# Four cross-attention and mixture-of-experts layers: layer 0's attention in a written TensorE order, and layer 1's setup and row gathers moved

## The chip, the cores and the metric

The kernel runs on one core of one Trainium2 chip. The metric is device time in microseconds of one execution; five runs of the kernel before gave 1270.8 to 1281.63 us with a median of 1277.07 us.

## The reference, cut to what matters

The input x is 4 batches of 512 tokens by 128 features, the context is 4 batches of 154 rows by 128, all float32. Four layers follow each other:

```python
for layer in range(4):
    x = x + attention[layer](layernorm(x), context)
    x = x + experts[layer](layernorm(x))
```

Layer 0's attention compares each token with the context rows, and projects four features:

```python
Sim  = (h @ w1)[:, :, None] + (c @ w2)[:, None, :] + einsum('bid,bjd->bij', h * w3, c) + b_sim
hq   = softmax(Sim, 2) @ c                       # per token
hc   = softmax(max(Sim, 2), 1) @ h               # one row per batch
out  = concat([h, hq, h * hq, h * hc]) @ W_qv + b_qv
```

Layer 1 is masked attention with 16 heads of 8 features; layers 2 and 3 have 16 heads of 64. Each expert layer has 8 experts with 512 or 256 hidden features. Layers 0, 2 and 3 send each token to the two experts with the highest gate logits and add the two results with softmax weights; layer 1 sends it to one, with a capacity of 321 tokens an expert.

## The kernel before, in words

x stays in SBUF, four tiles (one a batch) of 128 partitions by 4 groups of 128 tokens. Tokens are routed in two halves, batches 0 and 1 and batches 2 and 3.

**Layer 0's attention** (`attend_first`). `prepare(b)` normalises a batch, transposes it, multiplies it with the context (L1006) and makes the softmax's exponents on ScalarE (L1021). `tile_of` then transposes the probabilities (L1033, L1038; evacuated as `pm` and `pt`), multiplies them with the context (`hq`, L1041 and L1042), takes the maximum of the batch through a transpose and a matmul by ones (L1048, L1051, `m0`, `mall`), makes `md` (L1054), an exponent `ebt` (L1057) and the batch's row `hc` (L1060, L1061, `hd`, `hr`, `hc`, `wc` L1070), and projects the features in 12 matmuls (L1078, `res` L1081, added to x in L1083). The order of all this, on every engine, is found by a scheduler that lists instructions by its own estimate of times.

**The route of a half** (`route`, a generator that is advanced in steps): statistics and normalisation (L227 to L243; `rstd` L236 runs on GpSimd), transposes (L251), gating logits `lg` (L666, L672), the two best experts (`top`, `sel` L687), each token's rank within its expert by nine matmuls (L693, L695) and their copy `rk` (L697), and from it the row of a buffer in DRAM at which the token belongs, `su` (L717). The half's experts fill up to 23 blocks of 128 such rows (15 in layer 1), and `eb` (L745) is each block's expert. The tokens go there by indirect DMAs on GpSimd (L722), 16 in each half of a layer with two choices, 128 rows each. `row_transfers(n, behind)` (L641) issues the next n of these and makes them wait for one instruction, so that they spread over other work; in layer 0 it is called behind `pm`, `pt`, the copy `ft` of `hq`, and `res`, with n = 2.

**Experts** (`experts`). For each block the expert's weights are loaded by SP (L869, three buffers), and for each four blocks the tokens (L840), which wait until all scatters of their half have landed. Tokens are transposed (L850), multiplied with the first weights (L877), activated, multiplied with the second (L916) and stored (L928). A second half's route is advanced between the first half's blocks.

**Gather and combine.** When a half's blocks are stored, 16 indirect DMAs on GpSimd (L953) fetch each token's result rows; `combine` (L971) adds them to x with their weights. Layer 0's second half is gathered and combined beside layer 1's attention (`attend_all`): there the order of TensorE and ScalarE is written out by hand in periods, one for each of 16 tiles of 128 tokens (`narrow_period`; `nm` L294 is the maximum of six heads' scores, `probs` L308 their exponents, `short` L319 the last ScalarE step of a period, `pT` L264 an evacuation of transposed exponents). VectorE's order is the scheduler's. The combining of batches 2 and 3 is spread over the periods from the third tile on, two groups of 128 tokens in each.

**Layer 1's setup** (`layer1_setup`, L1088 on) makes block-diagonal weights through three 8-row transposes (L1099) and the transposed output projection (L1108). It is called right after layer 0's attention, so the scheduler may place it there. Its `prepare(0)`, which loads the mask `mi` and turns it to `madd` (L1122), is called after the first half's experts and gathers.

Of the kernel before, what the change touches and what calls it, by code (L numbers as in the profile page):

```python
# [29 lines left out]
NH = NT // 2  # L30
EPS = 1e-5
NEG = -1e20
BLK = (2 * NH + E - 1, NH + E - 1)
UPS = (2, 1, 1, 1)
NF = (4, 4, 2, 4)
PER = (1, 2, 2, 2)


# [9 lines left out]
def tile_xattn_moe_stack(ctx: ExitStack, tc: tile.TileContext, a: dict, out: bass.AP):  # L48
# [101 lines left out]
    for base, sign in ((0, 1), (D // H - 1, -1)):  # L150
# [17 lines left out]
    fill = const.tile([P, E, NH], F32, name="fill")  # L168
    nc.gpsimd.iota(
        fill, pattern=[[0, E], [P, NH]], base=0, channel_multiplier=0, allow_small_or_imprecise_dtypes=True  # L170
# [6 lines left out]
    nth = const.tile([1, BLK[0], E], F32, name="nth")  # L177
    nc.gpsimd.iota(
        nth, pattern=[[1, BLK[0]], [0, E]], base=0, channel_multiplier=0, allow_small_or_imprecise_dtypes=True
# [59 lines left out]
    def norm(src, found, pool=None):  # L239
        mv, rstd = found  # L240
        xn = (pool or xnp).tile([P, NI, D], F32, tag="xn", name="xn", bufs=3 if pool else 2)
        for i in range(NI):
            nc.vector.tensor_scalar(  # L243
                xn[:, i, :], src[:, i, :], mv[:, i, 0:1], rstd[:, i : i + 1], ALU.subtract, ALU.mult
            )
        return xn
# [23 lines left out]
    class Tile:  # L270
# [31 lines left out]
        def exp(self, g):  # L302
            if g == 0:
                self.pr = p2.tile([P, H, S2], F32, tag="probs", name="probs")
            for s in range(min(3, 8 - 3 * g)):
                for j in range(2):
                    h = self.at.heads(None, 3 * g + s, j)
                    nc.scalar.activation(  # L308
# [5 lines left out]
                    )  # L314

# [44 lines left out]
        def take_ends(self, engine):  # L360
            self.tails = p2.tile([self.rows, 4, P], F32, tag="tails", name="tails")
            copy(engine, self.tails.rearrange("p g q -> p (g q)"), self.q["ends"][0 : self.rows, :])
# [173 lines left out]
    def attention64(b, gather_x, wq, wk, wv, wo, add):  # L536
# [36 lines left out]
        def values_ends():  # L573
# [3 lines left out]
            for r in range(2):  # L577
                rows = slice(64 * r, 64 * r + 64)
                nc.tensor.matmul(q[rows, :], ct2[:, b], wv[:, r * 512 : (r + 1) * 512], start=True, stop=True)
# [6 lines left out]
            at.vt = at.vt.rearrange("p c s d -> p (c s d)")  # L586

# [35 lines left out]
    def rsm(name, *shape, dt=F32):  # L623
        return rt.tile([P, *shape], dt, tag=name, name=name)

    def top(lg):

        m = rt.tile([P, NH], F32, tag="m", name="m", bufs=4)
        nc.vector.tensor_reduce(m, lg, AX.X, ALU.max)
        eq = rt.tile([P, NH, E], F32, tag="eq", name="eq", bufs=4)  # L630
        nc.vector.tensor_tensor(eq, lg, bc(m, 2, E), ALU.is_equal)
        nc.vector.tensor_tensor(eq, eq, bc(rev_e, 1, NH), ALU.mult)
        r = rt.tile([P, NH], F32, tag="r", name="r", bufs=4)
        nc.vector.tensor_reduce(r, eq, AX.X, ALU.max)
        oh = rt.tile([P, NH, E], F32, tag="oh", name="oh", bufs=4)
# [5 lines left out]
    def row_transfers(n=2 * NH, behind=None):  # L641
# [9 lines left out]
    def route(layer, half, wg, bg, b2):  # L651

        lg = rsm("lg", NH, E)
        found = [stats(x[2 * half + k]) for k in range(B // 2)]
        yield
        xns = [norm(x[2 * half + k], found[k], rt) for k in range(B // 2)]
        yield  # L660
        xnTs = [transposed(xn) for xn in xns]
        yield
        for k, xnT in enumerate(xnTs):
            q = ps_tr()
            for i in range(NI):
                nc.tensor.matmul(q[:, i * E : (i + 1) * E], xnT[:, i * P : (i + 1) * P], wg, start=True, stop=True)  # L666
            o = lg[:, k * NI : (k + 1) * NI, :]
            qv = q[:, 0 : NI * E].rearrange("p (i e) -> p i e", i=NI)
            if bg is None:
                nc.vector.tensor_copy(o, qv)  # L670
            else:
                nc.vector.tensor_tensor(o, qv, bc(bg, 1, NI), ALU.add)  # L672
        yield
# [3 lines left out]
        sel = rsm("sel", NH + 1, E, dt=BF16)  # L677
        nc.vector.memset(sel[:, NH, :], 0.0)
        if layer == 1:
            nc.vector.tensor_copy(sel[:, 0:NH, :], oh1)  # L680
        else:
            yield
            lg2 = rsm("lg2", NH, E)
# [3 lines left out]
            nc.vector.tensor_tensor(sel[:, 0:NH, :], oh1, oh2, ALU.add)  # L687
# [3 lines left out]
        n = (NH + 1) * E  # L691
        q = ps_tr()
        nc.tensor.matmul(q[:, 0:n], before, sf, start=True, stop=False)  # L693
        for s in range(1, NH + 1):
            nc.tensor.matmul(q[:, s * E : n], ones_b, sf[:, 0 : n - s * E], start=False, stop=(s == NH))  # L695
        rk = rsm("rk", NH + 1, E)
        nc.vector.tensor_copy(rk, q[:, 0:n].rearrange("p (t e) -> p t e", t=NH + 1))  # L697
        tot = rk[:, NH, :]
        t3 = rsm("t3", E, NH)
        nc.vector.tensor_tensor(t3, bc(tot, 2, NH), fill, ALU.is_gt)  # L700
        nb = rsm("nb", E)
        nc.vector.tensor_reduce(nb, t3, AX.X, ALU.add)
        t4 = rsm("t4", E, E)
# [4 lines left out]
        base = rsm("base", NH, E)  # L708
        nc.vector.scalar_tensor_tensor(base, bc(first, 1, NH), float(P), rk[:, 0:NH, :], ALU.mult, ALU.add)
        slots = []  # L710
        for k, oh in enumerate(ohs):
            t5 = rsm("t5", NH, E)
            nc.vector.tensor_tensor(t5, base, oh, ALU.mult)
            sl = rsm(f"sl{k}", NH)
            nc.vector.tensor_reduce(sl, t5, AX.X, ALU.add)
            su = rsm(f"su{k}", NH, dt=U32)
# [17 lines left out]
        rows_due.extend(partial(scatter, t, su) for t in range(NH) for su in slots)  # L734
        yield

        nj = BLK[layer == 1]
        end = rt.tile([1, E], F32, tag="end", name="end")
        nc.vector.tensor_tensor(end, first[0:1], nb[0:1], ALU.add)
        t6 = rt.tile([1, BLK[0], E], F32, tag="t6", name="t6", bufs=1)  # L740
        nc.vector.tensor_tensor(t6[:, 0:nj, :], bc(end, 1, nj), nth[:, 0:nj, :], ALU.is_le)
        ef = rt.tile([1, BLK[0]], F32, tag="ef", name="ef")
        nc.vector.tensor_reduce(ef[:, 0:nj], t6[:, 0:nj, :], AX.X, ALU.add)
        eb = rt.tile([1, BLK[0]], I32, tag="eb", name="eb")
        nc.vector.tensor_scalar(eb[:, 0:nj], ef[:, 0:nj], float(E - 1), None, ALU.min)  # L745

        if layer == 1:

            le = rsm("le", NH, E)
            nc.vector.tensor_tensor(le, lg, bc(m1, 2, E), ALU.subtract)  # L750
            nc.scalar.activation(le, le, AF.Exp)
            ls = rsm("ls", NH)
            nc.vector.tensor_reduce(ls, le, AX.X, ALU.add)
            cw = rsm("cw", NH)
            nc.vector.reciprocal(cw, ls)
            rg = rsm("rg", NH, E)
            if half:
                nc.vector.tensor_tensor(rg, rk[:, 0:NH, :], bc(seen[0], 1, NH), ALU.add)
                nc.vector.tensor_tensor(rg, rg, oh1, ALU.mult)
            else:  # L760
                seen.append(tot)
                nc.vector.tensor_tensor(rg, rk[:, 0:NH, :], oh1, ALU.mult)
# [670 lines left out]
```

## Time and profile before

| | us |
|---|---|
| median of 5 runs (lowest, highest) | 1277.07 (1270.8, 1281.63) |
| the profiled execution's own time | 1273.25 |
| its span, first to last instruction | 1271.6 |
| TensorE busy | 1079.5 (85%) |
| VectorE busy | 731.1 (57%) |
| ScalarE busy | 565.5 (44%) |
| GpSimd busy | 253.0 (20%) |
| mean granted TensorE clock | 0.923 |

The profile is of one execution. Its time is 1.65 us longer than its span, and 3.82 us below the median of the five runs. A row of the trace gives the start and the duration of an instruction in us, engine (PE is TensorE, DVE is VectorE, ACT is ScalarE, POOL is GpSimd, SPq and POOLq their sequencers), line, operation, output and inputs, how many rows were taken together, and in brackets how long the engine was idle before it and which instruction's end ended that. The granted clock is the share of full speed that the throttle lets TensorE run at.

The stages as the trace has them: layer 0's attention and the first half's route until the first expert matmul at 104.06 us; layer 0's 46 expert blocks until 256 us; layer 1's first tiles, beside which the second half is gathered, until about 330 us; and the rest.

### The profile page before, as it was taken

To read this page: it belongs to the slowest core of one execution; us is meant where nothing else is said; L and a number is where in the kernel's file an instruction comes from. 1 tells how busy PE (TensorE), PEld (TensorE's weight loads), DVE (VectorE), ACT (ScalarE), POOL (GpSimd) and SP (SyncE) were. 2 spreads that over 40 slices of the span, in tenths; PEclk is the share of its full clock that TensorE was granted. 3 is DMA by queue.
4 is the path that set the end of the run, shared out by engine and by line. 5 is a ranking of instruction groups with operands and counts; after the bars stand their busy time and mean duration, and the time that the engine had idled before them with its cause. 6 is when DMAs were issued, how large, how long until landed. Compare 5 with 4: busy or idle time off the path is not lost.

```text
span 1271.6 us, 26318 instructions
## 1 busy us (share of the span) xinstructions
PE 1079.5 (85%) x9351; PEld 887.5 (70%) x9351; DVE 731.1 (57%) x2012; ACT 565.5 (44%) x2264; POOL 253.0 (20%) x281
## 2 busy tenths in 40 slices
PE   5777997977878788879999998965899999899890
PEld 3657997934334357778878777855778788789890
DVE  6565546557667764245666776424476676746352
ACT  2114332464454554446656565321656665632230
POOL 2041404023000100322000004045120000412334
PEclk8778999978998988989999999887899999999996
DMA  7024786621011213532112214454421111344762
GB/s 230 1 82 139 225 245 185 195 94 26 22 21 42 86 50 110 157 110 57 35 35 64 56 38 124 127 151 131 127 57 39 48 35 35 110 102 140 211 190 61
DMA packets 136064, 126.77 MB, mean 100 GB/s; under 512 B 12538, under 2 KB 115583, under 8 KB 135551
## 3 DMA queue, kind: packets, MB, share of 16 engines
q1 hardware_dynamic: 128767, 110.39, 30.7%
q0 software_dynamic: 7168, 14.69, 4.0%
q8 instruction: 77, 1.26, 0.4%
q14 instruction: 52, 0.43, 0.1%
HBM read 101.31 MB, written 23.72 MB: 98 GB/s over the span
## 4 chain that ended last, share of the span: by engine, by line
PE 58%; DVE 13%; DMA 9%; issue 8%; ACT 5%; POOL 4%; SPq 2%; POOLq 0%; DVEq 0%
PE sc L877 11%; PE av L916 6%; PE tr L371 6%; PE av L408 6%; PE sc L607 5%; PE tr L425 5%; DMA yg<-ybuf,su 3%; PE sc L592 3%; DVE nm L294 3%; ACT probs L308 3%; POOL yg L953 2%; PE sc L1175 2%; PE av L390 2%; DMA mi<-in_mask_Bx1xSxS_if 2%; PE tr L358 2%
## 5 line engine op out<-in xcount | busy, mean ns | idle before, releaser
L308 ACT ACTIVATE probs<-sc,nm 128x154 f32<-128x154 f32 x768 | 286.9, 402 | 162.3 <-DVE nm L294 162.1
L877 PE MATMUL sc<-tokT,w 128*128 128x128 f32 x1528 | 198.2, 283 | 10.2 <-DMA w<-in_up 4.2
L877 PEld LDWEIGHTS sc<-tokT,w 128*128 128x128 f32 x1528 | 186.0, 198 | 16.5 <-ACT eg L900 5.0
L294 DVE TENSOR_REDUCE nm<-sc 128x6 f32<-128x924 f32 x144 | 142.7, 1008 | 75.0 <-PE sc L607 49.1
L308 ACT ACTIVATION_READ_ACCUMULATOR probs<-sc,nm 128x1 f32 x768 | 167.9, 219 | 0.0
L916 PE MATMUL av<-w,hT 128*128 x1160 | 155.5, 279 | 4.1 <-DVE hT L905 3.2
L953 POOL DMA_INDIRECT yg<-ybuf,su x112 | 106.5, 951 | 250.5 <-ACT pT L267 61.0
L722 POOL DMA_INDIRECT buf<-xn,su x112 | 109.2, 975 | 218.7 <-DVE eb L745 96.4
L916 PEld LDWEIGHTS av<-w,hT 128*128 128x128 f32 x1160 | 142.0, 193 | 10.0 <-issue 5.8
L236 POOL TENSOR_TENSOR rstd<-ve,nhalf 128x4 f32<-128x4 f32 x32 | 32.9, 1031 | 543.0 <-DVE ve L234 423.9
L264 DVE COPY pT<-tr 128x512 f32<-128x512 f32 x160 | 107.0, 685 | 45.7 <-PE tr L371 42.1
L408 PE MATMUL av<-pT,vm 128*64 128x128 f32 (+1 forms) x1536 | 106.9, 286 | 22.2 <-DVE pT L264 21.9
L371 PE MATMUL tr<-ident,probs 128*128 128x128 f32 x768 | 122.4, 290 | 1.3 <-DVE rT L337 1.3
L371 PEld LDWEIGHTS tr<-ident,probs 128*128 128x128 f32 x768 | 85.5, 145 | 33.3 <-issue 22.2
L408 PEld LDWEIGHTS av<-pT,vm 128*64 128x64 f32 (+1 forms) x1536 | 63.9, 127 | 55.8 <-DVE pT L264 30.3
L900 ACT ACTIVATE eg<-sc,w 128x128 f32<-128x128 f32 x184 | 52.9, 368 | 88.3 <-PE sc L877 80.3
L607 PE MATMUL sc<-kT,qT 64*128 64x154 f32 x1024 | 87.1, 308 | 4.8 <-ACT probs L308 4.8
L905 DVE SCALAR_TENSOR_TENSOR hT<-sc,w,eg 128x128 f32<-128x128 f32 x184 | 56.2, 343 | 45.7 <-ACT eg L900 45.7
L607 PEld LDWEIGHTS sc<-kT,qT 64*128 64x128 f32 x1024 | 71.1, 188 | 15.7 <-issue 9.9
L592 PE MATMUL sc<-xnT,wq 128*128 128x128 f32 x512 | 73.0, 302 | 4.4 <-ACT probs L308 1.9
L592 PEld LDWEIGHTS sc<-xnT,wq 128*128 128x128 f32 x512 | 66.8, 211 | 9.9 <-issue 3.4
L925 DVE COPY ys<-av 128x256 f32<-128x256 f32 (+1 forms) x110 | 39.1, 356 | 49.8 <-PE av L916 49.3
(255 smaller groups left out, 1447.1 us busy)
## 6 DMA issues: line engine op xcount, KB each, us to landing
w<-in_up SPq DMA_DIRECT2D x46, 516.0 KB
w<-in_up SPq DMA_DIRECT2D x76, 258.0 KB
rep<-rd SPq DMA_DIRECT2D x64, 256.0 KB
tok<-buf SPq DMA_DIRECT2D x36, 256.0 KB
ybuf<-ys SPq DMA_DIRECT2D x58, 128.0 KB
w<-in_down SPq DMA_DIRECT2D x3, 2048.0 KB
w<-in_up SPq DMA_DIRECT2D x46, 128.0 KB
ybuf<-ys SPq DMA_DIRECT2D x52, 64.0 KB
```

Of the source, the lines that this page charges most:

```text
L264: return nc.vector.tensor_copy(o, i)
L294: nc.vector.tensor_reduce(self.at.heads(self.nm, g, n), self.sc[g][:, :, 0 : n * S2].rearrange("p j (s k) -> p j s k", s=n), AX.X, ALU.max ...
L308: nc.scalar.activation(self.pr[:, h, :], self.sc[g][:, j, s * S2 : (s + 1) * S2], AF.Exp, bias=self.nm[:, h : h + 1], accum_out=self.rs[:, ...
L371: nc.tensor.transpose(q[:, t * P : (t + 1) * P], self.pr[:, h, 0:P], ident)
L408: nc.tensor.matmul(av[rows, cols], v, self.pT[n][:, t, :], start=False, stop=last)
L425: nc.tensor.matmul(o[:, 0:D], self.aT[:, c, :], self.at.wo[:, c, :], start=(c == 0), stop=(c == self.nb - 1))
L592: nc.tensor.matmul(sc[:, c // 4, c % 4 * P : (c % 4 + 1) * P], wq[:, c * P : (c + 1) * P], at.xnT[:, i * P : (i + 1) * P], start=True, sto ...
L607: nc.tensor.matmul(sc[:, j, s * S2 : (s + 1) * S2], at.qT[i][rows, c, :], at.kT[rows, c, :], start=True, stop=True)
L722: ins = nc.gpsimd.indirect_dma_start(out=buf[half], out_offset=bass.IndirectOffsetOnAxis(ap=su[:, t : t + 1], axis=0), in_=xns[t // NI][:, ...
L877: nc.tensor.matmul(dst, w[:, b, at : at + P], xT, start=True, stop=True)
L916: nc.tensor.matmul(y[:, b * D : (b + 1) * D], hT[:, fc, :], w2[:, bass.ds(es[b], 1), fc, :].rearrange("p o d -> p (o d)"), start=(fc == 0) ...
L953: ins = nc.gpsimd.indirect_dma_start(out=yg[:, t, :], out_offset=None, in_=ybuf[half], in_offset=bass.IndirectOffsetOnAxis(ap=su[:, t : t ...
```

## The change

The halves stay what they were. `GROUPS` names the batches of each half, and sizes that were constants (8 groups a half, 23 or 15 blocks) are computed from it with the same values. What differs is this:

1. `tile_of` is a generator with two parts: up to `ebt`, and from `hc` on. The transpose of `m1` (L1048) is called ahead of the two `hq` matmuls.
2. `attend_first` writes TensorE's order out: the calls of attention parts and route steps are the order in which TensorE's instructions run. Layer 0's route normalises, transposes and gates batch by batch, and the first steps of the second half's route (batch 2) are called at the end of the attention. The other engines' order is still the scheduler's.
3. `row_transfers` takes 4 instead of 2 behind `pm`, `pt`, `ft` and `res`.
4. `layer1_setup` is called after the first half's expert blocks have been called.
5. In layer 1, the first tile's exponents each let 3 gathers go, and the second half's combining begins one period earlier. The parts of preparing the next batch are grouped differently over the periods: masks; values; normalisation; transposes with keys and queries (before: masks; normalisation with values; transposes; keys and queries).
6. Gathered rows lie in tiles of one batch (6 buffers) rather than of one half (2 buffers), and `combine` asks only for its own batch's gathers.
7. Buffer counts: the route's `xn` 4 for 3; `eq`, `lg2`, `t3`, `t4`, `base`, `t5`, `t7`, `le`, `rg` and `tails` have one buffer.

The core of the diff:

```diff
     def attend_first(layer, prepare, found):
-        tiles = [prepare(b, found[b]) for b in range(2)]
-        tiles[0](0)
-        tiles.append(prepare(2, found[2]))
-        tiles[1](0)
-        beside = Steps(route(layer, 0, *gates[layer])).step(3)
-        tiles.append(prepare(3, found[3]))
-        beside.step(5)
-        tiles[2](0)
-        beside.step(1)
-        tiles[3](0)
-        return beside.finish()
+        first, second = (Steps(route(layer, half, *gates[layer])) for half in range(2))
+        with tc.manual_schedule(engines={mybir.EngineType.PE}):
+            tiles = [prepare(b, found[b]) for b in range(2)]
+            tiles[0].finish()
+            tiles.append(prepare(2, found[2]))
+            tiles[1].step()
+            first.step()
+            tiles[1].finish()
+            tiles.append(prepare(3, found[3]))
+            tiles[2].step()
+            first.step(3)
+            tiles[2].finish()
+            first.step(2)
+            tiles[3].step()
+            first.step(2)
+            tiles[3].finish()
+            first.finish()
+            second.step()
+        return first.result, second
...
-            row_transfers(2, evac(pm, q))
+            row_transfers(4, evac(pm, q))
...
-            row_transfers(2, evac(pt, q[0:ST, :]))
-            hq = ps_av()
-            nc.tensor.matmul(hq, cm[:, b, :], pm, start=True, stop=False)
-            nc.tensor.matmul(hq, ctail[:, b, :], pt, start=False, stop=True)
+            row_transfers(4, evac(pt, q[0:ST, :]))
...
             nc.vector.tensor_reduce(m0, q[0:1, 0:P], AX.X, ALU.max)
+            hq = ps_av()
+            nc.tensor.matmul(hq, cm[:, b, :], pm, start=True, stop=False)
+            nc.tensor.matmul(hq, ctail[:, b, :], pt, start=False, stop=True)
             nc.tensor.matmul(q[:, P : P + 1], ones[0:1, :], m0, start=True, stop=True)
...
             nc.scalar.activation(ebt, md, AF.Exp, accum_out=es)
+            yield
...
     # route
-        xns = [norm(x[2 * half + k], found[k], rt) for k in range(B // 2)]
-        yield
-        xnTs = [transposed(xn) for xn in xns]
-        yield
+        for some in ([b] for b in batches) if layer == 0 else (batches,):
+            found = [stats(x[b]) for b in some]
+            if layer:
+                yield
+            new = [norm(x[b], f, rt) for b, f in zip(some, found)]
+            if layer:
+                yield
+            xnTs = [transposed(xn) for xn in new]
...
     # Tile.exp
+            if self.at.dh < 64 and self.at.first and self.i == 0:
+                row_transfers(3, ins)
...
-        got = [p2.tile([P, NH, D], F32, tag="yg", name="yg") for _ in routed[1]]
+            self.rows = [p2.tile([P, NI, D], F32, tag="yg", name="yg", bufs=6) for _ in range(choices)]
...
-            at.parts = ((masks,), (xn, values), (xnT,), (keys_queries,))
+            at.parts = ((masks,), (values,), (xn,), (xnT, keys_queries))
...
-                    step = nothing if (b, i) in ((0, 0), (0, 1), (2, 0)) else beside.step
+                    step = nothing if (b, i) in ((0, 0), (2, 0)) or layer > 1 and (b, i) == (0, 1) else beside.step
...
-        if layer < 3:
+        if 0 < layer < 3:
             prepare = setups[layer + 1]()
         first = Steps(experts(layer, 0, routed[0], w2)).step(2 // PER[layer])
...
-        got = gather(0, routed[0], stores)
+        got = gather(layer, 0, routed[0], stores)
         if layer < 3:
+            if layer == 0:
+                prepare = setups[1]()
             at = prepare(0, found)
```

## The prediction, as it was put on record

> **What bounds the kernel now.** I read the page's engine totals first, then the busy time of each engine by stage, then in the stages that the change touches the chain of waits and the rows of VectorE, GpSimd and SP.
>
> ```profile
> PE 1079.5 (85%) x9351; PEld 887.5 (70%) x9351; DVE 731.1 (57%) x2012; ACT 565.5 (44%) x2264; POOL 253.0 (20%) x281
> ```
>
> TensorE is the busiest, but its 85% is a mean. By stage (columns: busy time and instructions of PE, PEld, DVE, ACT, POOL, then the granted clock, DMA share, GB/s):
>
> ```profile
> 40.00:60.00 20.00, 12.50 (x65) 10.02 (x64) 13.66 (x51) 3.68 (x13) 2.01 (x2) 0.81 0.00 0
> 60.00:80.00 20.00, 14.78 (x69) 11.72 (x70) 12.18 (x55) 3.98 (x14) 5.03 (x5) 0.59 0.24 77
> ...
> 100.00:256.00 156.00, 145.65 (x1225) 139.71 (x1226) 86.00 (x326) 62.63 (x198) 32.72 (x34) 0.98 0.67 201
> 256.00:330.00 74.00, 56.05 (x363) 25.78 (x362) 47.42 (x112) 36.90 (x179) 17.31 (x18) 0.82 0.19 56
> 330.00:1272.00 942.00, 811.73 (x7447) 670.51 (x7447) 536.45 (x1325) 449.26 (x1833) 173.88 (x180) 0.94 0.32 86
> ```
>
> The reader is to see that layer 0's expert blocks (100 to 256 us) keep TensorE busy at nearly full clock, while layer 0's attention (A, to 104 us) and the start of layer 1 (C, 256 to 330 us) leave it idle and its clock at 0.59 to 0.82. The change works on A, on the blocks (B) and on C; after about 330 us its instructions stand as before but for small shifts.
>
> In A the end is set by a chain through VectorE and GpSimd:
>
> ```profile
> 70.03 0.23 DVE L697 COPY rk<-tr 128x72 f32<-128x72 f32 x1
> ...
> 73.14 0.22 DVE L717 CAST su<-sl 128x8 uint32<-128x8 f32 x2
> ...
> 73.60 1.19 POOL L722 DMA_INDIRECT buf<-xn,su  x1 [15.72 <-DVE eb L745]
> 75.09 0.96 POOL L722 DMA_INDIRECT buf<-xn,su  x1 [0.30 <-issue]
> ...
> 95.25 1.34 POOL L722 DMA_INDIRECT buf<-xn,su  x1 [2.24 <-DVE res L1081]
> 96.89 0.96 POOL L722 DMA_INDIRECT buf<-xn,su  x1 [0.30 <-issue]
> ...
> 102.16 1.99 PE L850 MATMUL tr<-ident,tok 128*128 128x128 f32 x8 [7.08 <-DMA tok<-buf]
> 104.06 4.16 PE L877 MATMUL sc<-tokT,w 128*128 128x128 f32 x23
> ```
>
> Ranks (70.03) give slots (73.14), slots let 16 scatters go at one per 0.96 + 0.30 = 1.26 us, and TensorE, done with the attention, idles 7.08 us for the tokens. So in A only what moves the first scatter or the pace of the sixteen moves the end.
>
> **The change, part by part.** A. The changed program's instruction order on each engine shows what is queued ahead of what.
>
> Batch 0 gains 1 us: `madd` (L1122) holds VectorE until its mask lands at 30.57, ahead of `md`, which then starts at 30.99 for a chain that ends x0 at 41.3; in the new order `md` stands ahead of it and could start when `mall` ends at 29.5. I count 0.9 of those 1.5 us: x0 at 40.4.
>
> Batch 1 loses it again. Its four probability transposes (1.06 us at half clock) ran under batch 0's chain; now they stand behind batch 0's projection (12 matmul pairs: 20 passes took 3.1 us from 50.82, 2.5 from 84.47) and batch 2's transposes and scores (0.66 and 1.21 at full clock, 1.06 and 2.42 at half). From the projection's end at 39.87 − 0.9 = 39.0 that is 39.0 + 0.66 + 1.21 + 2 × 0.66 = 42.2 for the start of `hq` at full clock, against 41.19: x1 at 55.4 + 1.0 = 56.4, or 57.7 if half of the stretch runs at half clock. From x1 VectorE's new queue to the last `xn` (statistics 0.86, aggregates 0.36, score addition 0.86, `pt` 0.69, `sm` 0.80, `xn` 1.1, small ones, and `rstd` 1.03 on GpSimd) is about 6 us, then transposes, copy and gating 3: the second `lg` at 65 to 67, against 65.42.
>
> Then the ranks. The nine rank matmuls (0.5 us) ran as soon as `sel` was there (TensorE had idled 4.11 us for it). Now they stand behind batch 2's `hc` matmuls and 12 projection pairs, whose `wc` is made in the middle of the routing arithmetic, 3.5 us after `lg`. 3.5 + 2.5 to 3.1 + 0.5 puts `rk` 6.5 to 7.1 us after `lg`, with `res` (0.69) beside: 71 to 74.4, against 70.03. I take 72.5.
>
> From `rk` to the first `su`: before, 3.1 us (70.03 to 73.14). Now 26 VectorE rows stand between: `pm`, the residual of batch 2, `cT`, `ft` at 0.69 each, four statistics 0.86, four aggregates 0.36, four `xn` 1.1, and small ones of 0.15 to 0.33; in all 8.7 us. Some of these wait: `hd` stands ahead of `su` and needs eight transposes, both `hq` matmuls (1.1 us each at full clock, 2.07 at half), `ebt`, eight transposes of `comb` and L1060 (1.05 or 1.86). That chain on TensorE is 6.2 us at full clock and 11.3 at half, plus about 1 us from `hd` to `su`. So `su` comes 8.7 us (full) to 12.3 us (half) after `rk`; at the clock of the rows 72 to 84 (0.91, 0.52, 0.63) about 9. That gives `su` at 81.5, between 79.7 (71 + 8.7) and 86.7 (74.4 + 12.3).
>
> [...]
>
> The scatters: with four rather than two behind each evacuation they run without a hold once `su` is there; `res` comes 4 to 6 us after `su`, while the last four of sixteen are due 15 us after it. First start 81.5 + 0.4 = 81.9 (before 73.60), last 81.9 + 19.2 = 101.1 (before 96.89, 2.24 of hold and a `rstd` of 1.04 among them, which now stands behind): +4.2. Four transposes rather than eight stand ahead of the first expert matmul: −0.3. **A: +3.9 us, between +1.9 and +9.** The fill is gone: `wc` at about 82, 12 pairs, the experts' output biases (1.13) and batch 2's gating end near 90, so TensorE waits some 16 us, to 102.16 + 4.2 = 106.4, instead of 7.08.
>
> B. 1 us of the second half's first transposes and gating moved from the blocks into A's idle; four setup transposes (0.22 to 0.30 each, 0.6 in all beside PEld) moved in: −0.4 net. Three small loads on SP (`wo_r`, `gamma_r`, `beta_r`) now stand among the weight loads, each behind a setup transpose; two weight loads in flight hide that: nothing, and 0.5 if that cover fails. The second half's scatters start behind block 4 rather than 7 (135.24 before, three blocks of 2.68 us), so SP no longer waits here:
>
> ```profile
> 160.71 0.34 SPq L869 DMA_DIRECT2D w<-in_up  x1
> 163.00 0.92 SPq L840 DMA_DIRECT2D tok<-buf  x2
> 164.03 0.44 SPq L928 DMA_DIRECT2D ybuf<-ys  x1
> 165.05 0.36 SPq L869 DMA_DIRECT2D w<-in_up  x1
> ```
>
> The weight load at 165.05 (4.66 us to landing) came about 2 us late; with the buffers ahead of it I count 1 of that. **B: −1.5, between −3 and 0.**
>
> C. The blocks' last store lands at 263.71, yet the first gather starts behind a `pT`:
>
> ```profile
> 269.74 1.00 POOL L953 DMA_INDIRECT yg<-ybuf,su  x1 [46.87 <-DVE pT L264]
> ...
> 286.65 0.94 POOL L953 DMA_INDIRECT yg<-ybuf,su  x1 [5.40 <-DVE ve L234]
> ...
> 296.41 0.95 POOL L953 DMA_INDIRECT yg<-ybuf,su  x1 [0.30 <-issue]
> ```
>
> Now nine may go behind the first tile's exponents, at 263.74, 6.0 us earlier; sixteen at 1.26 with a `rstd` end at 284.0 and their data (2.5 us on) at 286.6, against 298.9. But all sixteen pairs of combining now stand in VectorE's queue ahead of the third tile's second maximum (`nm`, at 282.27 before), on which ScalarE's exponents wait. It goes to 286.6 + 1 = 287.6: 5.3 us late. The fourth tile's maximum stood at 299.51 behind the last gather; it comes a clean period after, 287.6 + 11.2 = 298.8: 0.7 early. The fourth part (transposes with keys and queries, in one period rather than two) adds about 1 there. **C: 0, between −4 and +3**; 6.1 us of VectorE's waits for `yg` bound what can be gained at the start, and the four periods between the first five `short` (262.63, 276.31, 291.51, 310.23, 321.42) exceed the last of them, 11.2 us, by 2.5, 4.0, 7.5 and 0, 14 in all.
>
> The rest: same work, `t5` and others with one buffer on an engine that runs in order anyway: 0 ± 1. **Sum: 3.9 − 1.5 + 0 = +2.4 us**: 1275.7 on the profiled execution's own time of 1273.25, and, since that lies 3.8 below the median of the five runs (1277.07), 1279.5 on the scale of the median.
>
> **Rivals.** 1. Slower: the slots' chain. If the clock stays at half from the ranks on, `su` comes at 86 or later, the last scatter at 86.4 + 19.2 = 105.6, A at +8.5 or more, and neither B nor C gives it back. For it: 0.50 in the rows 60 to 72, and transposes and waits follow each other in the new order. Against: 0.91 at 72 to 76 and 1.00 from 84 on. Price 8 to 10 us: about 1286. It decides from `su` later than 86.
>
> 2. Faster: the second half's combining gets out of VectorE's way. If the maximum of the third tile isn't held (gathers faster than VectorE gets to them), the periods lose up to 8 of their 14 us of excess, B gives its 3, and A loses only 2: 1277.1 − 8 − 3 + 2 = 1268. For it: gathers can start 6.0 us earlier and 9 waits on `yg` are named. Against: the order puts 32 combines ahead of that maximum.
>
> 3. It doesn't do what it says: VectorE's order, still the scheduler's, sets the slots' time and A is unchanged; then B alone remains: 1275.5.
>
> **Numbers.** 0.5% (6.4 us) is about what a measurement of this kernel can tell from no change. The forecast, +2.4, and rival 3 are within it: 0.38 and 0.03. Rival 1: 0.32. Rival 2: 0.27. The range takes in rival 2's place at its low end and A's and C's bounds together at the high (1277.1 + 9 + 3 = 1289): 1267 to 1289, with 0.9 of rival 1 and most of rival 2 inside. Forecast alone: 1271 to 1283.
>
> **What would show it.** Right: `rk` at 71 to 74, `su` about 9 us later, first scatter near 82, last near 101, first expert matmul near 108; no hold of SP before the second half's token loads; first gather 6 us after the last expert store's issue and not behind `pT`; third tile's second maximum late, fourth on time. Wrong: a first scatter before 78 (VectorE's rows overlap better than summed), or periods of 11 us from the second on (C gains), or 13 and more beyond the fifth (C loses more).

## The result

The changed kernel took 1278.35 us (median of 44 runs), the kernel before 1276.08 (86 runs): ratio 1.0017, 95% interval 1.0004 to 1.0029, that is 2.2 us slower, between 0.5 and 3.7. The forecast was +2.4 us. The profiled execution took 1276.87 us with a span of 1275.1, 3.6 and 3.5 above those of before.

The changed kernel's engine totals, and its stages cut at the same events (first expert matmul, first maximum of layer 1, and 74 us on), in the columns of the prediction:

```profile
PE 1082.3 (85%) x9351; PEld 891.0 (70%) x9351; DVE 730.5 (57%) x2012; ACT 564.9 (44%) x2264; POOL 252.4 (20%) x281
```

```profile
40.00:60.00 20.00, 16.48 (x91) 13.34 (x91) 13.07 (x49) 4.15 (x14) 1.01 (x1) 0.83 0.00 0
60.00:80.00 20.00, 17.78 (x98) 13.37 (x96) 14.96 (x70) 5.23 (x18) 2.01 (x2) 0.81 0.01 2
107.00:257.00 150.00, 145.01 (x1204) 138.43 (x1202) 85.86 (x330) 62.34 (x198) 33.15 (x34) 0.98 0.67 206
257.00:331.00 74.00, 52.56 (x371) 24.47 (x369) 48.19 (x110) 36.95 (x179) 17.46 (x18) 0.89 0.19 56
331.00:1276.00 945.00, 815.59 (x7447) 673.20 (x7447) 537.67 (x1327) 448.88 (x1833) 173.72 (x180) 0.94 0.31 86
```

The work is the same. TensorE has more of it before 80 us (17.78 of 20 us busy at a clock of 0.81, against 14.78 at 0.59) and then waits longer. The timeline of the slots' chain in the changed kernel shows why:

```profile
73.53 0.22 DVE L719 COPY rk<-tr 128x72 f32<-128x72 f32 x1
80.54 0.14 DVE L739 CAST su<-sl 128x8 uint32<-128x8 f32 x1
...
80.99 1.19 POOL L744 DMA_INDIRECT buf<-xn,su  x1 [2.71 <-DVE hc L1104]
82.49 0.96 POOL L744 DMA_INDIRECT buf<-xn,su  x1 [0.30 <-issue]
...
100.17 0.96 POOL L744 DMA_INDIRECT buf<-xn,su  x1 [0.30 <-issue]
...
105.52 1.09 PE L872 MATMUL tr<-ident,tok 128*128 128x128 f32 x4 [13.37 <-DMA tok<-buf]
106.40 1.06 PE L260 MATMUL tr<-ident,xn 128*128 128x128 f32 x4
107.28 4.92 PE L899 MATMUL sc<-tokT,w 128*128 128x128 f32 x31
```

Ranks come at 73.53 (before 70.03), slots 7.0 us after them (before 3.1), the sixteen scatters run without a hold, and TensorE idles 13.37 us for the tokens. SP's token loads and the gathers in the changed kernel:

```profile
158.88 0.34 SPq L891 DMA_DIRECT2D w<-in_up  x1
159.53 0.93 SPq L862 DMA_DIRECT2D tok<-buf  x2
```

```profile
266.73 0.99 POOL L983 DMA_INDIRECT yg<-ybuf,su  x1 [42.35 <-DMA ybuf<-ys]
...
286.80 1.07 POOL L983 DMA_INDIRECT yg<-ybuf,su  x1 [0.53 <-DVE xn L252]
```

The first gather now starts when the blocks' stores have landed, no longer behind a `pT`, and the last one 9.6 us earlier than before (296.41). Yet the stage is as long as it was: VectorE's maxima stand behind the combines, as these rows of its timeline show (`nm` of the third tile's second group of heads is the last row). There are 16 combines in all, eight pairs, and not the 32 of the prediction and of one expectation. In both kernels a period that combines is given four groups of 128 tokens, not two as the text ahead of the prediction has it, and so eight combines.

```profile
283.14 0.35 DVE L1007 SCALAR_TENSOR_TENSOR x<-yg,wb,x 128x128 f32<-128x128 f32 x1 [0.77 <-DMA yg<-ybuf,su]
...
289.40 0.35 DVE L1007 SCALAR_TENSOR_TENSOR x<-yg,wb,x 128x128 f32<-128x128 f32 x1 [0.74 <-DMA yg<-ybuf,su]
...
290.41 1.11 DVE L303 TENSOR_REDUCE nm<-sc 128x6 f32<-128x924 f32 x1
```

The same maximum in the kernel before:

```profile
282.27 1.12 DVE L294 TENSOR_REDUCE nm<-sc 128x6 f32<-128x924 f32 x1 [0.43 <-PE sc L1175]
```

VectorE's queue holds TensorE too, as VectorE took its list in order: `rT`, whose transpose TensorE had done at 267.94, ran at 273.07, after three combines before which VectorE was idle 2.28, 0.98 and 0.26 us for gathered rows. In the changed kernel TensorE stands idle for two evacuations that VectorE has listed among the combines:

```profile
273.39 0.91 PE L382 MATMUL tr<-ident,probs 128*128 128x128 f32 x4 [5.01 <-DVE rT L348]
...
286.58 0.65 PE L419 MATMUL av<-pT,vm 128*32 128x128 f32 x8 [4.28 <-DVE pT L273]
```

Behind the second of them come the scores of the third tile's second group, which end at 289.96, so that its maximum has its input only 0.45 us before it starts. The first five ends of a period (`short`) in the changed kernel:

```profile
264.65 0.55 ACT L330 COPY short<-probs 128x416 f32<-128x416 f32 x1
282.61 0.54 ACT L330 COPY short<-probs 128x416 f32<-128x416 f32 x1
297.77 0.55 ACT L330 COPY short<-probs 128x416 f32<-128x416 f32 x1
312.56 0.55 ACT L330 COPY short<-probs 128x416 f32<-128x416 f32 x1
323.76 0.54 ACT L330 COPY short<-probs 128x416 f32<-128x416 f32 x1
```

The second period grew from 13.7 to 18.0 us and the fourth shrank from 18.7 to 14.8; the third has 15.2 in both.

### The profile page after: what moved, and what is told of

The parts are those of the page before. It is cut to its first block, busy times and chain, and to the rows that moved or that the text cites. A ratio compares the mean times of both kernels' runs of the same rounds, so it can differ in the third digit from the quotient of the medians.

```text
span 1275.1 us, 26305 instructions
## 1 busy us (share of the span) xinstructions
PE 1082.3 (85%) x9351; PEld 891.0 (70%) x9351; DVE 730.5 (57%) x2012; ACT 564.9 (44%) x2264; POOL 252.4 (20%) x281
## 4 chain that ended last, share of the span: by engine, by line
PE 60%; DVE 16%; DMA 9%; issue 6%; ACT 5%; POOL 4%; SPq 1%; POOLq 0%; DVEq 0%; ACTq 0%
PE sc L899 11%; PE av L938 7%; PE tr L382 6%; PE av L419 6%; PE sc L619 5%; PE tr L436 5%; DMA yg<-ybuf,su 3%; PE sc L604 3%; DVE nm L303 3%; ACT probs L317 3%; PE sc L1213 2%; PE av L401 2%; POOL yg L983 2%; POOL buf L744 2%; PE tr L369 2%
## 5 line engine op out<-in xcount | busy, mean ns | idle before, releaser
L899 PE MATMUL sc<-tokT,w 128*128 128x128 f32 x1528 | 200.9, 285 | 6.9 <-DVE tokT L98 2.3
L983 POOL DMA_INDIRECT yg<-ybuf,su x112 | 107.0, 955 | 240.9 <-DMA ybuf<-ys 62.4
L273 DVE COPY pT<-tr 128x512 f32<-128x512 f32 x160 | 107.0, 685 | 45.2 <-PE tr L382 41.4
```

Source lines behind the costliest of these rows:

```text
L273: return nc.vector.tensor_copy(o, i)
L899: nc.tensor.matmul(dst, w[:, b, at : at + P], xT, start=True, stop=True)
L983: ins = nc.gpsimd.indirect_dma_start(out=yg[:, i % NI, :], out_offset=None, in_=ybuf[half][0 : most_blocks(layer, half) * P, :], in_offset ...
```

## The experiments

Theory: the ranks' place behind batch 2's projection costs time ahead of the first expert matmul; layer 1's first periods are long because VectorE stands in its queue for gathered rows while the exponents wait for its maxima, and the change leaves that as it was. Rivals: the written TensorE order itself is what costs; the half clock costs whatever the order; the difference lies in the regrouped parts.

The stages of each profiled execution, in us, where P1, P5 and P16 are the ends of the first, fifth and sixteenth period of layer 1 (`short`):

| kernel | first expert matmul | from there to layer 1's first maximum | P1 to P5 | P5 to P16 | P16 to the end |
|---|---|---|---|---|---|
| before | 104.1 | 151.1 | 58.8 | 148.5 | 801.7 |
| before, again2 | 110.7 | 151.0 | 56.9 | 154.9 | 804.5 |
| changed | 107.3 | 149.9 | 59.1 | 152.2 | 799.1 |
| e_rank | 101.7 | 150.9 | 62.2 | 153.1 | 801.4 |
| e_noorder | 107.1 | 150.7 | 59.4 | 151.8 | 799.6 |
| e_parts | 107.0 | 151.6 | 59.9 | 148.7 | 802.9 |
| e_tie | 107.4 | 150.8 | 55.3 | 154.7 | 800.4 |
| e_spread2 | 103.2 | 152.6 | 48.1 | 151.7 | 806.2 |
| e_spread_norank | 107.4 | 150.2 | 48.8 | 152.6 | 800.2 |
| e_spread_newparts | 103.6 | 150.5 | 46.6 | 149.9 | 800.4 |

Four more profiles, from a chip on which every kernel took longer, are told of with their runs.

**Ranks ahead of batch 2's projection (e_rank).**

```diff
+            first.step(2)
             tiles[2].finish()
-            first.step(2)
             tiles[3].step()
```

> The changed kernel with the rank and slot steps of the first half's route called ahead of batch 2's projection instead of behind it; nothing else differs. Theory A (the ranks' place behind batch 2's projection, and the VectorE rows that this puts between ranks and slots, delay the slots): ranks near 70, slots near 73, sixteen scatters from 73.5 without a hold, last near 94, first expert matmul near 99 to 101 instead of 107.28, and the whole time 6 to 8 us below the changed kernel, 4 to 5 us below the kernel before. Rival B (the half clock and VectorE's load delay the slots whatever their place, or the attention's own end becomes the bound): first expert matmul at 104 or later and less than 3 us gained on the changed kernel.

Measured: 1277.42 us against 1280.26 before, ratio 0.998 (0.9953 to 1.0007). Its timeline:

```profile
69.54 0.23 DVE L719 COPY rk<-tr 128x72 f32<-128x72 f32 x1
...
72.00 0.15 DVE L739 CAST su<-sl 128x8 uint32<-128x8 f32 x1
```

```profile
95.80 1.23 PE L260 MATMUL tr<-ident,xn 128*128 128x128 f32 x4 [6.86 <-DVE xn L252]
98.18 1.87 PE L687 MATMUL tr<-wg,xnT 128*128 128x8 f32 x8 [1.15 <-DVE xnT L98]
99.90 1.09 PE L872 MATMUL tr<-ident,tok 128*128 128x128 f32 x4
100.79 1.06 PE L260 MATMUL tr<-ident,xn 128*128 128x128 f32 x4
101.67 2.49 PE L899 MATMUL sc<-tokT,w 128*128 128x128 f32 x14
```

Slots come 2.5 us after the ranks, scatters run from 73.02 to 93.32, and the first expert matmul starts at 101.67, 5.6 us earlier than in the changed kernel and just past theory A's 99 to 101: the second half's first transposes and gating, written ahead of the tokens' transposes, now wait for a `rstd` that stands behind the sixteen scatters. So the ranks' place is the cause of the late slots, not the clock: from 60 to 72 us it was 0.73 in the changed kernel, and the same matmuls took as long in both (the gating 1.06 us in each, `ebt`'s eight 1.76 there and 1.84 here). Against the changed kernel's 1.0017 the ratio is 0.4% lower, with intervals that meet at 1.0004 to 1.0007; theory A's 6 to 8 us on the whole time is more than can be shown, since the periods P1 to P5 took 3.1 us longer here.

**TensorE's order left to the scheduler (e_noorder).**

```diff
-        with tc.manual_schedule(engines={mybir.EngineType.PE}):
+        if True:
```

> The changed kernel with the attention's calls in the same order, but TensorE's order left to the scheduler. Theory A (the order of the calls, not the written order, puts the ranks behind batch 2's projection: the scheduler lists them there too): first expert matmul at 106 to 108, time within 1.5 us of the changed kernel. Rival B (writing TensorE's order out makes it wait): first expert matmul at 104 or earlier, 3 us below the changed kernel.

Measured: ratio 0.9989 (0.9964 to 1.0013); ranks, scatters (81.01 to 100.21) and first expert matmul (107.06) stand as in the changed kernel. Theory A: it is the order in which the program calls the steps that puts the ranks where they are. Writing the order out did nothing measurable to this stage. The ratio is 0.3% below the changed kernel's, more than theory A's 1.5 us, but the two intervals overlap.

**Parts as before (e_parts).**

```diff
-            at.parts = ((masks,), (values,), (xn,), (xnT, keys_queries))
+            at.parts = ((masks,), (xn, values), (xnT,), (keys_queries,))
```

> The changed kernel with the parts of layer 1's next batch grouped as in the kernel before. Theory A (the regrouped parts, transposes with keys and queries in one period, lengthen layer 1's later periods by 3.7 us): from the fifth to the sixteenth end of a period 148.5 us as before instead of 152.2, time 3 to 4 us below the changed kernel. Rival B (that difference belongs to single executions and clock, not to the grouping): 151 to 153 us and no difference in time.

Measured: 148.7 us from P5 to P16, as theory A has it, but a ratio of 1.0029 (0.9999 to 1.0059), not lower. The kernel before, with these parts, took 148.5 in one execution and 154.9 in another. The runs below with the old parts took 151.7 and 152.6 there (e_spread2, e_spread_norank), the one with the new parts 149.9 (e_spread_newparts). So the 3.7 us that the two first profiles differ by there can't be put down to the grouping. Rival B's 151 to 153 us were not met, but its reading, that the difference belongs to single executions, fits all these numbers.

**Combining tied to the maxima (e_tie).** Each combine waits for the last maximum written ahead of it, so the scheduler can no longer list all of them first; eight combines fall into each of two periods.

```diff
+            latest[:] = [nc.vector.tensor_reduce(
...
-            nc.vector.scalar_tensor_tensor(xi, yg[:, i, :], cw[:, t : t + 1], xi, ALU.mult, ALU.add)
+            ins = nc.vector.scalar_tensor_tensor(xi, yg[:, i, :], cw[:, t : t + 1], xi, ALU.mult, ALU.add)
+            if layer == 0 and half == 1:
+                wait_for(ins, latest, "behind the maximum of the period")
...
-                    step = nothing if (b, i) in ((0, 0), (2, 0)) or layer > 1 and (b, i) == (0, 1) else beside.step
+                    step = nothing if (b, i) in ((0, 0), (0, 1), (2, 0)) else beside.step
```

> The changed kernel with each combining of layer 0's second half made to wait for the last maximum written ahead of it, and started a period later as before, so that in VectorE's order the 32 combines stand behind the third tile's maxima and are spread over two later periods. Theory A (VectorE stands in its queue for gathered rows and so delays the maxima on which the exponents wait): the second to fourth periods go from 18.0, 15.2 and 14.8 us to 11 to 13 each, 8 to 12 us gained. Rival B (those periods are long for other reasons: TensorE's clock, transposes, the first tiles' evacuations; or the combining lengthens later periods by as much): less than 3 us gained.

Measured: ratio 0.9987 (0.996 to 1.0014). The ends of the first five periods on ScalarE:

```profile
265.63 0.54 ACT L330 COPY short<-probs 128x416 f32<-128x416 f32 x1
276.61 0.55 ACT L330 COPY short<-probs 128x416 f32<-128x416 f32 x1
288.00 0.55 ACT L330 COPY short<-probs 128x416 f32<-128x416 f32 x1
304.25 0.55 ACT L330 COPY short<-probs 128x416 f32<-128x416 f32 x1
320.96 0.54 ACT L330 COPY short<-probs 128x416 f32<-128x416 f32 x1
```

Periods two and three are 11.0 and 11.4 us (18.0 and 15.2 in the changed kernel): the combines in VectorE's queue, with 6.9 us of its waits for gathered rows in the changed kernel, did hold them. But the fourth and fifth, which now have eight combines each with a batch's statistics, and the next batch's normalisation, transposes and keys in one of them, are 16.2 and 16.7 (14.8 and 11.2). VectorE was busy 13.43 of the 16 us from 288 to 304. P1 to P5 is 3.8 us shorter, not theory A's 8 to 12. Theory A's mechanism holds and rival B's second half too: the work was pushed into later periods. An even spread was tried next.

**Spread, with old parts and early ranks (e_spread), or in two periods (e_all).** On top of e_tie: the edits of e_rank and e_parts; in e_spread the combining is called from the second period on as in the changed kernel, with one step of four combines a period.

```diff
                     def after(b=b, i=i, step=step):
-                        step()
+                        if layer > 1 or (b, i) not in ((0, 1), (0, 2), (0, 3), (1, 0)):
+                            step()
```

> The changed kernel with three edits together: the ranks ahead of batch 2's projection, layer 1's parts grouped as before, and the second half's combining tied to the last maximum written ahead of it, two groups of 128 tokens (four combines) in each of four periods. Theory A (what each edit gave alone in its own stage adds up: 5.6 us at the first expert matmul, 3.7 us between the fifth and the sixteenth end of a period, and the second to fourth periods near 11 to 13 us instead of 48 in all): 12 to 18 us below the changed kernel, ratio to the kernel before 0.988 to 0.993. Rival B (VectorE's queue has the same work to do in layer 1's first periods wherever it stands, so what one stage gains another gives back): sixteenth end of a period at 472 to 476 us again, ratio 0.996 to 1.001.

> As the run with the combining spread, but eight combines in each of two periods (fourth and fifth) with the two batches' statistics behind them. Theory A: second and third periods near 11, fourth and fifth 14 to 16, 8 to 14 us below the changed kernel, 4 us above the spread one. Rival B (the number of combines in a period does not matter, the sum does): as the spread one within 2 us.

Measured: 1347.05 us, ratio 1.002 (0.9991 to 1.0048), and 1352.23, ratio 1.0059 (1.0031 to 1.0086). But the kernel before took 1343.51 on that chip, 5% more than elsewhere. The trace of e_all shows what is different (VectorE's waits: what it waited for, us in total, times, longest):

```profile
DVE ys L948 <- remote: 28.8, 4, 12.3
...
DVE nm L303 <- remote: 11.4, 2, 8.3
...
DVE res L1121 <- remote: 10.4, 1, 10.4
```

VectorE and ScalarE stood idle for single stretches, VectorE's of up to 13.7 us (`ys`, in the run with the setup in its old place), whose releaser the trace calls remote. The traces of all four kernels profiled on this chip have them, and no other trace has. Some fell into the very periods that were asked about (23.5 and 26.1 us for the third), so these two runs decide nothing about the theories. On this chip the spread kernel is not shown to be faster than the kernel before; what it gains is shown only on the two other chips below.

**The kernel before again (e_again), and the setup in its old place (e_setup),** beside those two.

> The kernel before, unchanged, profiled a second time, to see how far the stages of one execution repeat. Theory A (stages repeat within about 1 us): first expert matmul 104 to 105, from there to layer 1's first maximum 150 to 152 us, from the fifth to the sixteenth end of a period 147.5 to 149.5, the rest of the span after that 800 to 803. Rival B (stages differ by 2 us and more between executions of the same kernel, so that ledgers from single profiles say little): at least one of these outside.

> The changed kernel with layer 1's setup called right after layer 0's attention, as before. Theory A (the move of the setup is worth next to nothing: its transposes lie beside weight loads in either place): first expert matmul within 1 us of 107.28, from there to layer 1's first maximum 149.5 to 151.5 us. Rival B (in its old place its loads and transposes stand in the first half's way): first expert matmul 1 us or more later, or the blocks 1 us or more shorter.

```diff
-        if 0 < layer < 3:
+        if layer < 3:
             prepare = setups[layer + 1]()
...
-            if layer == 0:
-                prepare = setups[1]()
```

Measured: before 1344.44 us, first expert matmul at 110.50, 154.3 us to layer 1's first maximum; setup in its old place 1356.26 us, 108.99 and 153.5. Both have the unexplained stretches (in the latter one of 4.7 us on ScalarE ahead of layer 1), but none ahead of the first expert matmul. So the 110.50 counts, and contradicts theory A's 104 to 105; the last `res` held the scatters 3.94 us (2.24 in the first profile). For the setup, 108.99 lies outside theory A's 1 us, but the ranks were already 1.7 us late (75.22 against 73.53). With one profile, whose later stages are disturbed, the setup's place is not settled.

**Spread again on another chip (e_spread2), and before again (e_again2).**

> The kernel with the ranks ahead, the old parts and the combining spread, run again, because the four kernels run together before showed VectorE and ScalarE idle for single stretches of up to 10 us without a releaser in the trace, in the kernel before too. Theory A (without such stretches the three gains add up): first expert matmul 100 to 103, second to fourth periods 11 to 14 us each, sixteenth end of a period 455 to 462 us, ratio to the kernel before 0.988 to 0.993. Rival B (what one stage gains another gives back): sixteenth end of a period above 468, ratio 0.996 to 1.002.

> The kernel before, profiled once more beside the spread one. Theory A (stages repeat within about 1 us where no such stretches occur): first expert matmul 103.5 to 104.6, blocks to layer 1's first maximum 150.5 to 151.7, first to fifth end of a period 58 to 60, fifth to sixteenth 147.5 to 149.5. Rival B (a stage differs by 2 us or more between executions): at least one outside.

Measured: spread 1266.02 us against 1279.22 before, ratio 0.9893 (0.986 to 0.9926): 13.7 us faster than the kernel before. Its periods:

```profile
263.29 0.54 ACT L330 COPY short<-probs 128x416 f32<-128x416 f32 x1
274.27 0.55 ACT L330 COPY short<-probs 128x416 f32<-128x416 f32 x1
286.11 0.54 ACT L330 COPY short<-probs 128x416 f32<-128x416 f32 x1
300.04 0.55 ACT L330 COPY short<-probs 128x416 f32<-128x416 f32 x1
311.41 0.55 ACT L330 COPY short<-probs 128x416 f32<-128x416 f32 x1
```

11.0, 11.8, 13.9 and 11.4 us, 48.1 in all against 59.1 in the changed kernel. VectorE waits for no gathered row in this stage any more. Its combines run in the third to the sixth period here, so the last four lie behind P5; the gain is still there at the end of the sixteenth period, at 463.1 (changed 475.9). That is a little later than theory A's 455 to 462, as the first expert matmul (103.2) is later than its 100 to 103; the ratio is inside its bounds.

The repeated profile of the kernel before took 1287.22 us, longer than the eleven executions beside it (1276.16 to 1284.95), and contradicts theory A of its own expectation: first expert matmul at 110.72, 6.6 us later than in the first profile, with the same instructions. On GpSimd (idle before and its releaser in brackets):

```profile
95.62 1.04 POOL L236 TENSOR_TENSOR rstd<-ve,nhalf 128x4 f32<-128x4 f32 x1 [1.17 <-DVE ve L234]
101.17 1.34 POOL L722 DMA_INDIRECT buf<-xn,su  x1 [4.50 <-DVE res L1081]
102.81 0.95 POOL L722 DMA_INDIRECT buf<-xn,su  x1 [0.30 <-issue]
```

and the clock in the same execution (the eighth number is the granted clock):

```profile
76.00:80.00 4.00, 3.55 (x11) 1.51 (x11) 1.59 (x4) 0.69 (x2) 3.08 (x4) 0.50 0.82 261
80.00:84.00 4.00, 4.00 (x20) 3.62 (x18) 1.12 (x5) 0.77 (x3) 3.02 (x4) 0.50 0.64 238
84.00:88.00 4.00, 4.00 (x10) 1.65 (x10) 1.07 (x3) 0.30 (x2) 2.87 (x3) 0.54 0.15 49
...
96.00:100.00 4.00, 4.00 (x20) 3.85 (x19) 1.57 (x6) 0.00 (x0) 0.66 (x1) 0.50 0.00 0
```

The first profile had 0.63 and then 1.00, up to 96 us:

```profile
80.00:84.00 4.00, 4.00 (x14) 2.12 (x13) 1.64 (x6) 0.30 (x2) 2.94 (x4) 0.63 0.35 131
84.00:88.00 4.00, 4.00 (x32) 3.22 (x30) 1.68 (x5) 1.14 (x2) 3.08 (x4) 1.00 0.15 50
```

The ranks were 1.6 us late already (71.60 against 70.03); most of the rest comes with the last scatters. In the kernel before, they wait for `res` of batch 3, whose matmuls ran at half clock here (0.50 from 96 to 100 us; four by `wqv` took 1.06 us, and 0.61 in the first profile; the last `res` held the queue 4.50 us, and 2.24 in the first profile). In the changed kernel all sixteen run free, and five profiles of kernels with its ranks' place, all without the unexplained stretches, have the first expert matmul at 107.0 to 107.4.

**Which edit carries the gain (e_spread_norank, e_spread_newparts).** The spread kernel with the ranks put back behind the projection, and with the changed kernel's parts.

> The kernel that beat both (ranks ahead, old parts, combining spread) with the ranks put back behind batch 2's projection. Theory A (most of its gain is layer 1's first periods, 11 us there; the ranks' place is worth 3 to 5 us at the first expert matmul): first expert matmul near 107, first to fifth end of a period 47 to 50 us, ratio to the kernel before 0.990 to 0.995. Rival B (the gain is the ranks' place): ratio 0.998 or more.

> The kernel that beat both with the changed kernel's grouping of parts (transposes with keys and queries in one period). Theory A (normalisation and transposes of the next batch fall into the period that also has the keys, VectorE's queue then holds the maxima): fourth period 15 to 17 instead of 13.9 us, later periods 152 instead of 148 to 152, ratio 0.990 to 0.995. Rival B (with the combining spread the grouping makes no difference): first to fifth end of a period 47 to 49 us and the ratio within 0.1% of 0.989.

Measured: 1267.2 against 1275.18, ratio 0.9926 (0.9898 to 0.9953), and 1264.87 against the same 1275.18, ratio 0.9919 (0.9892 to 0.9947). Without early ranks the first expert matmul is back at 107.36 and P1 to P5 stays at 48.8: the spread, with the old parts, makes the changed kernel faster than before without the early ranks. The old parts alone had gained nothing (e_parts); no run has the spread alone. With the changed kernel's parts the fourth period is 15.3 us rather than 13.9, as theory A has it, but with the old parts and late ranks it is 15.5, so the grouping isn't shown to be the reason. P5 to P16 is 149.9 rather than theory A's 152, and P1 to P5 is 46.6, the shortest of all. The three ratios' intervals overlap; which of the three kernels is the fastest stays open. All three beat both kernels.

## Why the prediction was right, point by point

**Layer 0's attention and first scatters.** x0 ended at 40.3 (predicted 40.4) and x1 at 57.65 (56.4 to 57.7), the second `lg` stood at 65.52 (65 to 67), `rk` at 73.53 (72.5 taken, 71 to 74.4), `su` at 80.54 (81.5), first and last scatter at 80.99 and 100.17 (81.9 and 101.1), the first expert matmul at 107.28 (108.0). The one term that was off in size is `rk` to `su`: 7.0 us, not 9, below even the 8.7 summed for VectorE alone, since in the timeline VectorE rows start before the one ahead ends (`first` at 76.84 with 0.21, the next row at 76.96). The clock from 72 to 80 was 0.97 and 0.89, so rival 1 (half clock, `su` at 86 or later) had not its condition. That waits of TensorE bring the half clock, as its reason has it, no run shows: here it was 0.50 from 68 to 72 with no idle above 0.9 us between 62 and 72. Two small sums of the prediction don't come out as written: by its own terms A's lower bound is 2.1, not 1.9, and B is −1.4, not −1.5. e_rank shows the mechanism, the ranks' place, and e_noorder that the written order was not it.

What the prediction did not see: +3.2 us at the first expert matmul is against one profile of the kernel before, and two others have 110.50 and 110.72, later than the changed kernel's 107.28. The first was a favourable one (its time, 1273.25, lies 2.8 below the median of 86 runs), the one with 110.72 an unfavourable one. What the change costs here on average, and even whether it costs, is therefore not known from these traces.

**The expert blocks.** The second half's scatters started at 131.91 (135.24) and the token loads at 159.53 (163.00), as forecast, and the stage was 1.2 us shorter (1.5 forecast). But it lies between 149.9 and 152.6 in all profiles without the unexplained stretches, 150.2 to 151.6 in four that have the same blocks as the changed kernel. A gain of 1 us is not shown.

**Layer 1's first periods.** Forecast 0, measured +0.3 (59.1 for 58.8). Relative to the stage's start, the first gather came 5.0 us earlier (6.0 forecast), the third tile's second maximum 6.1 late (290.41 against 282.27, less 2.0 of the start; 5.3 forecast), the fourth tile's 0.3 late (301.81 against 299.51; 0.7 early forecast). The mechanism was right in the main: the gathers' gain is spent in VectorE's queue. What the prediction left out is that the queue also holds the evacuations TensorE waits for (5.01 and 4.28 us), and by them the scores of that maximum, and it counted 32 combines where there are 16. Rival 2's condition, maxima that aren't held, is what the spread kernels bring about: 10 to 12 us less than in the kernel before, where the rival had 8.

**The rest.** Forecast 0 ± 1; the two profiles differ by +3.7 from P5 to P16 and by −2.5 from there to the end. Repeated profiles of the kernel before differ by 6.4 and 2.8 in the same stretches, so neither can be put down to the change.

**Chances.** The median moved by 0.17%, inside the 0.5% that had 0.41. That the sum of +2.4 met the 2.2 measured is partly luck: its terms are right against one execution, whose stages repeat less well than the sum suggests. Against that execution the stages of the changed kernel's profile add up to +3.5. Which stage the 2.2 us of the medians belong to is not shown.

## What to carry to other kernels

Where a scheduler orders an engine, the order of the calls can decide, as it did here, what stands ahead of a small critical instruction; look at that engine's list for what was put between two links of a chain. Earlier data doesn't help an engine that takes its list in order, as VectorE did here, and has been given the consumers earlier still: tie such fill work behind the step that others wait for, and spread it evenly, since eight combines in each of two periods gave back in the later periods most of what the earlier ones gained. Profile the same kernel twice before a stage's difference of a few microseconds is put down to a change.

## What the runs showed of the hardware

The granted clock of one stage is not the same in two executions of one kernel: 0.63 and 1.00 from 80 to 88 us in one, 0.50 and 0.54 in another, which ended the stage 6.6 us later. What made them differ no run shows. One chip took 5% longer for the four kernels that ran on it, with VectorE and ScalarE idle in single stretches that the trace calls remote (VectorE's up to 13.7 us, one of ScalarE's 4.7); their cause was not found.
